# Last recurrent step of a two-layer graph network: gates batch by batch, and half of a batch moved from the TensorE turn to the DRAM path

## The chip, the cores and the metric

The kernel runs on one core of one Trainium2 chip. The metric is the device time of one execution in microseconds; 0.2% of it is about 3.6 us. Names used: PE is TensorE (PEld its weight loads), DVE is VectorE, ACT is ScalarE, SP is the engine whose queue issues every DMA of this kernel.

## The reference

Sixteen batches of 1024 nodes with 128 features go through two layers. The second layer is a gated recurrent update with five steps. Everything is float32. Cut to what matters here:

```python
# layer 1
h = relu(layernorm(x1))
for _ in range(5):
    m = adj @ h                                   # the same matrix for "in" and "out"
    z = sigmoid(concat(m, m) @ w3.T + b3 + h @ u3.T + bu3)
    r = sigmoid(concat(m, m) @ w4.T + b4 + h @ u3.T + bu3)
    hv = tanh(concat(m, m) @ w5.T + b5 + (r * h) @ u5.T + bu5)
    h = (1 - z) * h + z * hv
out = x1 + h
```

x1 is layer 0's output, kept in DRAM until it is needed for the last line.

## The kernel before

**Tiling.** Sixteen batches are worked on in four quads of four (batches 0 to 3, ..., 12 to 15). Two quads are in flight at any time, and each step of one quad has two stages. The aggregation `m = adj @ h` (`aggregate`, matmuls on L504) goes through all four batches at once, with sums that save multiplications. Then come the gates (`gates`, L799), on transposed data: features lie on the 128 partitions, nodes run along the row. A unit is one batch's half of 512 nodes. `hT` holds the state h transposed, `mT` the aggregated messages transposed.

**Gates.** They run for a pair of batches at a time: pair A is the first two batches of a quad, pair B the last two. For a pair's four units, first all four r gates (products with W4A and U3, sigmoid, `r * h` on DVE), then all four z gates (one more product into the same PSUM bank, sigmoid), then the four updates `update` (L835: products with W5A and U5, tanh, then DVE). Without `finish` an update takes three DVE operations: `hv - h`, times z, plus h. All products are issued on L808, with 512 columns; each shows as two pieces in the trace.

**Order.** Every instruction goes through `pin`, so each engine works in exactly the order in which the program is written. `put(key, piece)` hangs a piece of other work on a named place, and `place(key)` runs it there. Places of an aggregation are the numbers 1 to 49 (after so many of its products), those of the gates have names such as `Ar0` or `Bz3`: pair, gate, unit. Loads and stores hung on places go into SP's queue in that order. An SP entry that must wait, for data or for a free buffer, holds up all that stands behind it.

**The last step.** Nothing follows it, so the state is added to x1 and stored. It has two ways from transposed to natural layout:

- Through DRAM: DVE transposes 32x32 squares within the partitions (L669, tile `sq`), one 512 KB store writes them to a scratch (`fn<-sq`), four loads of 128 KB fetch the blocks in natural order (`ho<-fn`, `natural_from`), and DVE adds the blocks to x1 (`xt<-xt,ho`, L241, two strided additions). Batches 12 and 13 (pair A) go this way. `final_outputs` (L1009) puts the loads and the additions in pair B's places: loads at Br0 and Br2, additions with the store to `out` at Bz1 and Bz3.
- By TensorE: `finish` (L1027) multiplies 128 columns of `hT` at a time by the identity (L1043, tile `pf`), and DVE adds the bank to x1. Batches 14 and 15 (pair B) go this way. In pair B `1 - z` is computed as a second sigmoid (L831), and `(1 - z) * h` is done during the z gates (L832), so that an update needs only two DVE operations. The last unit's update is split in two halves of 256 columns.

`flip` has three buffers (`sq`, `ho`), `pre` has four (x1 tiles), `ps_g` four PSUM banks; `ps_m` has tag a with two, b and c with one. Output 11, of the quad before, also lands in this step: its load at Ar0, its addition at Az1, its store at Az2. The x1 loads of batches 12 to 15 sit at Ar1, Ar2, Ar3 and Br1.

Of the kernel before, what the change touches and what calls it, by code (L numbers as in the profile page):

```python
# [8 lines left out]
F32 = mybir.dt.float32  # L9
# [4 lines left out]
P = 128  # L14
# [82 lines left out]
def tile_two_gnn_layers(  # L97
# [30 lines left out]
    def dma(out, in_):  # L128
        pin(nc.sync.dma_start(out=out, in_=in_))

    def by_slots(ap):
        return ap.rearrange("(p c) d -> p c d", c=NC)
# [33 lines left out]
    def flat(t):  # L166
        names = "abcd"[: len(t.shape) - 1]
        return t.rearrange(f"p {' '.join(names)} -> p ({' '.join(names)})")
# [68 lines left out]
    def sub(o, a, b):  # L237
        pin(nc.vector.tensor_sub(o, a, b))  # L238

    def add(o, a, b):  # L240
        pin(nc.vector.tensor_add(o, a, b))  # L241
# [405 lines left out]
    def scratch_for(kind, nm):  # L647

        scratch = dram.tile([P, N], F32, tag=f"{kind}_{nm}", name=f"{kind}_{nm}")
        return scratch, scratch.rearrange("(a y) (k f) -> k y a f", a=NSQ, k=NSQ)  # L650
# [4 lines left out]
    def flip_tile(nm):  # L655
        return flip.tile([P, NSQ, NC, SQ], F32, tag="sq", name=nm)

    def squares_of_half(sq, g):
        return sq[:, :, bass.ts(g, CH), :].rearrange("p k j e -> p j k e")

    def transposed_half(hT, g):
        return hT[:, bass.ts(g, HALF)].rearrange("p (j k e) -> p j k e", j=CH, k=NSQ)
# [10 lines left out]
    def natural_from(blocks, hN):  # L673

        for k in range(NSQ):
            dma(by_blocks(hN, k), blocks[k])
# [31 lines left out]
    def put(k, *pieces):  # L708
        fixed.setdefault(k, []).extend(pieces)

    def place(k):
        for piece in fixed.pop(k, ()):
            piece()
# [82 lines left out]
        return rest  # L796


    def gates(mT, hT, nm, key, then, finish=None):  # L799

        def view(t, u):
            return t[u[0]][:, bass.ts(u[1], HALF)]

        def multiply(bank, w, moving, start, stop):
            pin(
                nc.tensor.matmul(  # L808
                    bank, w_sb[:, w, :], moving, start=start, stop=stop, skip_group_check=True
                )  # L810
            )

        banks, rh, z = {}, {}, {}
        for k, u in enumerate(UNITS):
            tag = f"{nm}_{u[0]}{u[1]}"
            pg = ps_g.tile([P, HALF], F32, tag="pg", name=f"pr_{tag}")
            multiply(pg, W4A, view(mT, u), True, False)
            multiply(pg, U3, view(hT, u), False, True)
            r = work.tile([P, HALF], F32, tag="r", name=f"r_{tag}")
            pin(nc.scalar.activation(r, pg, AF.Sigmoid, bias=bsum[:, 1:2]))  # L820
            pin(nc.vector.tensor_mul(r, r, view(hT, u)))
            banks[u], rh[u] = pg, r
            place(f"{key}r{k}")
        for k, u in enumerate(UNITS):
            multiply(banks[u], W3A, view(mT, u), False, True)
            tag, h = f"{nm}_{u[0]}{u[1]}", view(hT, u)
            z[u] = work.tile([P, HALF], F32, tag="z", name=f"z_{tag}")
            pin(nc.scalar.activation(z[u], banks[u], AF.Sigmoid, bias=bsum[:, 0:1]))
            if finish:
                rest = work.tile([P, HALF], F32, tag="hv", name=f"rest_{tag}", bufs=3)  # L830
                pin(nc.scalar.activation(rest, banks[u], AF.Sigmoid, bias=nb3, scale=-1.0))  # L831
                pin(nc.vector.tensor_mul(h, h, rest))  # L832
            place(f"{key}z{k}")

        def update(u, part):  # L835

            tag = f"{nm}_{u[0]}{u[1]}_{part.start}"
            h = view(hT, u)[:, part]
            pg = ps_g.tile([P, HALF], F32, tag="pg", name=f"pv_{tag}")[:, part]
            multiply(pg, W5A, view(mT, u)[:, part], True, False)  # L840
            multiply(pg, U5, rh[u][:, part], False, True)
            hv = work.tile([P, HALF], F32, tag="hv", name=f"hv_{tag}", bufs=3)[:, part]
            pin(nc.scalar.activation(hv, pg, AF.Tanh, bias=bsum[:, 2:3]))
            if finish:
                pin(nc.vector.tensor_mul(hv, hv, z[u][:, part]))
            else:
                pin(nc.vector.tensor_sub(hv, hv, h))
                pin(nc.vector.tensor_mul(hv, hv, z[u][:, part]))
            pin(nc.vector.tensor_add(h, h, hv))

        if not finish:
            for k, u in enumerate(UNITS):
                update(u, slice(0, HALF))
                if k % NH == NH - 1:
                    then(u[0])
            return
        updates = [(u, slice(0, HALF)) for u in UNITS[:-1]]
        updates += [(UNITS[-1], slice(k * BLK, (k + 1) * BLK)) for k in range(2)]
        for k, (u, part) in enumerate(updates):
            update(u, part)  # L860
            if k >= 2:
                finish(*updates[k - 2])
        for late in updates[-2:]:
            finish(*late)


    state = {}
# [9 lines left out]
    def step(i, loads_at=(period(4), period(5), "Ar0", "Ar2"), early_places=GATE_PLACES):  # L877
# [24 lines left out]
        if final:  # L902
            st["x1"] = []

            def load_x1(k):
                x1 = x_tile(f"1_{quad * Q + k}")
                dma(x1, x1s[quad * Q + k])
                st["x1"].append(x1)

            for k, places in enumerate(((None, 10, 13), (12, 24, 27), (26, 39, 41), ("Ar0", "Az1", "Az2"))):  # L910
                for piece, at in zip(outputs[(quad - 1) * Q + k], places):
                    if at is not None:
                        put(at, piece)
            for k, at in enumerate(("Ar1", "Ar2", "Ar3", "Br1")):
                put(at, lambda k=k: load_x1(k))
        if source is not None:
            loads_of_next(source, loads_at)
# [27 lines left out]
        if last:  # L945
            outputs.update({quad * Q + k: output(quad * Q + k, Later(lambda n, k=k: ready[k][n])) for k in range(Q)})
            if quad == quads - 2:
                put("Bz1", outputs[quad * Q][0])
        for a, key in enumerate("AB"):
            pair = slice(2 * a, 2 * a + 2)  # L950
            if final and a == 1:
                for k, (load, rest) in enumerate(final_outputs(quad, st, stored)):
                    put(f"Br{2 * k}", load)
                    put(f"Bz{2 * k + 1}", rest)
            gates(
                [mT[:, 2 * a + k] for k in range(2)],
                hT[pair],
                f"{nm}{key}",
                key,
                turn(2 * a),  # L960
                finish=finish(quad, hT[pair], st) if final and a == 1 else None,
            )
        if final:
            st["quad"], st["blocks"] = None, None
            return
        st["step"] += 1
        st["blocks"] = [stored[k] for k in range(Q)]
        if last:
# [36 lines left out]

    def h0_of(quad):
        return Later(lambda k: h0_blocks[quad * Q + k])

    def final_outputs(quad, st, stored):  # L1009
        for k in range(2):  # L1010
            box = {}

            def load(k=k, box=box):
                box["h"] = flip_tile(f"ho_{quad * Q + k}")
                natural_from(stored[k], box["h"])

            def rest(k=k, box=box):
                x1 = st["x1"][k]
                view = x1.rearrange("p j (a e) -> p a j e", e=SQ)
                for g in range(NH):  # L1020
                    js = bass.ts(g, CH)
                    add(view[:, :, js], view[:, :, js], box["h"][:, :, js])
                dma(by_slots(out[quad * Q + k]), x1)

            yield load, rest

    def finish(quad, hT, st):  # L1027

        count = [0]

        def run(u, part):
            i, g = u
            x1 = st["x1"][2 + i]
            n = (part.stop - part.start) // P
            first = g * CH + part.start // P
            bank = ps_m.tile(
                [P, n, D], F32, tag="abac"[count[0] % 4], name=f"pf_{i}_{first}",
                bufs=2 - count[0] % 2,
            )
            count[0] += 1  # L1040
            for j in range(n):
                pin(
                    nc.tensor.matmul(  # L1043
                        bank[:, j, :], hT[i][:, bass.ts(first + j, P)], ident, start=True, stop=True
                    )
                )
            slots = slice(first, first + n)
            add(x1[:, slots], bank, x1[:, slots])
            dma(by_slots(out[quad * Q + 2 + i])[:, slots], x1[:, slots])

        return run


    firsts = [slotwise(nat[:, k]) for k in range(Q)]
# [163 lines left out]
```

## Time and profile before

| what | value |
|---|---|
| median of 3 runs | 1781.39 us (1778.98 to 1782.17) |
| the profiled execution | 1784.15 us |
| its span on the core | 1782.4 us, mean granted clock 0.998 |
| first product of the last step's gates | 1732.04 us |
| last addition on DVE ends | 1779.14 us |

All times below and in the prediction are microseconds from the start of the span. The last step's gates and outputs fill the final 50 us, in which the engines were busy as follows (PE, DVE and ACT, in us):

| stretch | PE | DVE | ACT | granted clock |
|---|---|---|---|---|
| 1732.04 to 1749.20 (pair A) | 17.16 | 9.97 | 7.93 | 1.00 |
| 1749.20 to 1764.80 (pair B: r, z, three updates' products) | 15.60 | 12.74 | 9.45 | 1.00 |
| 1764.80 to 1770.30 | 0.02 | 2.66 | 0.69 | 0.82 |
| 1770.30 to 1782.40 (turning, last update, last stores) | 8.06 | 6.80 | 0.95 | 0.78 |

The table is read by stretch: PE is full in the first two, and in the last two no engine is.

SP's queue in this step, with the start of each entry (an entry that waits starts when its wait ends):

| start | entry |
|---|---|
| 1718.80 to 1721.76 | last three ring loads of the aggregation |
| 1724.86 | store of output 10 |
| 1725.25 | four loads of output 11's blocks |
| 1727.51 to 1729.84 | x1 of batches 11 to 14 |
| 1741.75 | store of output 11 |
| 1750.56 | scratch store of batch 12 |
| 1755.99 | scratch store of batch 13 |
| 1756.40 to 1758.14 | four loads of batch 12's blocks |
| 1758.66 | x1 of batch 15 |
| 1759.09 to 1760.51 | four loads of batch 13's blocks |
| 1763.19, 1768.93 | stores of outputs 12 and 13 |
| 1773.51, 1776.31, 1778.48, 1778.90, 1779.38 | stores of outputs 14 and 15, in parts |

### The profile page before, as it was taken

What the parts mean: (1) busy time and instruction counts of PE and PEld (TensorE: products, weight loads), DVE (VectorE), ACT (ScalarE), POOL (GpSimd) and SP (SyncE); (2) the same over time, 40 slices, a digit from 0 to 9 for tenths busy, and PEclk for the clock granted to TensorE, in tenths of its full rate; (3) what the DMA queues carried; (4) which work ended last, traced back from release to release, by engine and by line L of the source; (5) the groups of instructions that cost most, each with busy time, mean ns of one, the idle gap of its engine ahead of it and who ended that gap; (6) DMA issues with size and microseconds to landing.
All of it is one profiled execution on the core that took longest, in us unless ns stands there. A gap on an engine that the chain in (4) does not pass through costs nothing.

```text
span 1782.4 us, 21452 instructions
## 1 busy us (share of the span) xinstructions
PE 1764.8 (99%) x6450; PEld 1204.2 (68%) x6450; DVE 1372.3 (77%) x2807; ACT 902.4 (51%) x1971; POOL 59.3 (3%) x41
## 2 busy tenths in 40 slices
PE   9999999999999999999999999999999999999997
PEld 4557666588586675858866758576675857658574
DVE  6778979777879688887697968768677776867776
ACT  5246555544555565554455554544445454544543
POOL 3101000000000000000000000000000000000000
PEclk9999999999999999999999999999999999999999
DMA  7489886589495865849849668594775948567593
GB/s 253 158 310 308 238 247 211 179 233 266 120 307 187 270 210 180 260 132 278 253 152 283 212 202 277 164 303 156 221 232 158 295 142 260 189 205 249 162 318 118
DMA packets 168866, 396.36 MB, mean 222 GB/s; under 512 B 18480, under 2 KB 86960, under 8 KB 168752
## 3 DMA queue, kind: packets, MB, share of 16 engines
q1 hardware_dynamic: 168752, 395.00, 70.7%
q8 instruction: 52, 0.85, 0.2%
q14 instruction: 62, 0.51, 0.1%
HBM read 314.18 MB, written 80.74 MB: 222 GB/s over the span
## 4 chain that ended last, share of the span: by engine, by line
PE 84%; DVE 7%; DMA 6%; POOL 1%; ACT 1%; issue 1%; SPq 0%; DVEq 0%; POOLq 0%
PE a L504 23%; PE c L504 12%; PE b L504 6%; DMA ring<-rd 4%; PE a_a L504 3%; PE pr_3B L808 2%; PE pr_2B L808 2%; PE pr_1B L808 2%; PE pr_2A L808 2%; PE pr_1A L808 2%; PE pr_3A L808 2%; PE pr_0B L808 2%; PE pr_4A L808 2%; PE pr_0A L808 2%; PE a_a L620 2%; PE pv_3B L808 2%
## 5 line engine op out<-in xcount | busy, mean ns | idle before, releaser
L504 PE MATMUL a<-ring,big 128*128 128x256 f32 x1120 | 288.3, 380 | 2.9 <-ACT Z L523 2.1
L523 ACT COPY Z<-a 128x256 f32<-128x256 f32 x480 | 177.6, 371 | 196.4 <-PE a L504 196.1
L241 DVE TENSOR_TENSOR Z<-Z,taps 128x512 f32<-128x512 f32 (+1 forms) x264 | 144.6, 554 | 167.1 <-ACT taps L523 166.8
L504 PE MATMUL c<-ring,little 128*128 128x256 f32 x960 | 246.8, 379 | 0.7 <-ACT Z L523 0.5
L504 PEld LDWEIGHTS a<-ring,big 128*128 128x128 f32 x1120 | 211.6, 190 | 41.9 <-issue 8.1
L241 DVE TENSOR_TENSOR mT<-mT,Z 128x1024 f32<-128x1024 f32 x154 | 188.4, 1223 | 24.7 <-ACT Z L523 19.4
L504 PEld LDWEIGHTS c<-ring,little 128*128 128x128 f32 x960 | 181.8, 190 | 27.0 <-ACT Z L523 1.7
L523 ACT COPY taps<-c 128x256 f32<-128x256 f32 x280 | 103.7, 370 | 117.1 <-PE c L504 111.9
L504 PE MATMUL b<-ring,big 128*128 128x256 f32 x560 | 143.8, 379 | 0.4 <-DMA ring<-rd 0.4
L504 PE MATMUL a<-resident,little 128*128 128x256 f32 x560 | 143.9, 379 | 0.0
L504 PE MATMUL a<-ring,little 128*128 128x256 f32 x560 | 143.7, 379 | 0.0
L504 PEld LDWEIGHTS b<-ring,big 128*128 128x128 f32 x560 | 106.3, 190 | 15.2 <-DMA ring<-rd 0.8
L504 PEld LDWEIGHTS a<-resident,little 128*128 128x128 f32 x560 | 106.2, 190 | 14.9 <-ACT Z L523 0.3
L504 PEld LDWEIGHTS a<-ring,little 128*128 128x128 f32 x560 | 106.4, 190 | 14.5
L669 DVE STREAM_TRANSPOSE sq<-hT_all 128x512 f32<-128x512 f32 x156 | 101.2, 686 | 0.0
L401 ACT COPY big<-nat 128x512 f32<-128x512 f32 x132 | 80.6, 614 | 0.1
L523 ACT COPY taps<-b 128x256 f32<-128x256 f32 x140 | 52.1, 372 | 55.5 <-PE b L504 54.6
L238 DVE TENSOR_TENSOR little<-little,big 128x256 f32<-128x256 f32 x154 | 65.4, 425 | 6.7
L238 DVE TENSOR_TENSOR little<-big 128x256 f32<-128x256 f32 x154 | 64.3, 417 | 0.0
L238 DVE TENSOR_TENSOR little<-big,little 128x256 f32<-128x256 f32 x154 | 64.2, 417 | 0.0
L241 DVE TENSOR_TENSOR little<-big 128x256 f32<-128x256 f32 x154 | 64.0, 415 | 0.3 <-ACT big L401 0.2
L523 ACT COPY mT<-a 128x256 f32<-128x256 f32 x80 | 29.8, 372 | 48.1 <-PE a L504 47.9
(267 smaller groups left out, 2915.0 us busy)
## 6 DMA issues: line engine op xcount, KB each, us to landing
ring<-rd SPq DMA_DIRECT2D x440, 512.0 KB, 6.3
fn<-sq SPq DMA_DIRECT2D x78, 512.0 KB, 3.5
nat<-fn SPq DMA_DIRECT2D x256, 128.0 KB, 6.6
x1d<-xt SPq DMA_DIRECT2D x16, 512.0 KB, 5.3
sqt<-ft SPq DMA_DIRECT2D x16, 512.0 KB, 6.5
xt<-x1d SPq DMA_DIRECT2D x16, 512.0 KB, 7.1
xt<-in_x_dram SPq DMA_DIRECT2D x15, 512.0 KB, 4.6
ho<-fn SPq DMA_DIRECT2D x56, 128.0 KB, 6.9
```

The source lines that it names most:

```text
L238: pin(nc.vector.tensor_sub(o, a, b))
L241: pin(nc.vector.tensor_add(o, a, b))
L401: return [lambda i=i: pin(nc.scalar.copy(made_of(k, i), part(a, b, i))) for i in range(2)]
L504: nc.tensor.matmul(bank, l, right[:, c, :], start=opens and c == 0, stop=c == SB - 1, skip_group_check=True,)
L523: pin(nc.scalar.copy(to, bank))
L620: nc.tensor.matmul(bank, left[:, c, :], right[c // SB][:, c % SB], start=p in (1, 2, 5) and c == 0, stop=c == CH - 1, skip_group_check=True,)
L669: pin(nc.vector.transpose(squares_of_half(sq, g), transposed_half(hT, g)))
L808: nc.tensor.matmul(bank, w_sb[:, w, :], moving, start=start, stop=stop, skip_group_check=True)
```

## The change

The last step of the last quad no longer uses `gates`, `finish` and `final_outputs` but a function of its own, `last_gates`. `gates` keeps only the case without `finish`; its other uses are the same instructions as before.

- The order is batch by batch rather than pair by pair: r of batch 12, z of batch 12, r of batch 13, update of batch 12, z of 13, update of 13, then r and z of 14, its update, r and z of 15, its update. Between r and z of batch 15 stand no other products.
- All four batches compute `1 - z` as a second sigmoid and `(1 - z) * h` right after z, so all updates have two DVE operations. The result of that sigmoid goes to `nat`, which is free by then.
- Batches 12 and 13 and the first half of batch 14 go through DRAM. The half takes one transpose, one scratch store of 256 KB in 512-byte pieces and four loads of 64 KB, also in 512-byte pieces. The second half of 14 and both halves of 15 are turned by TensorE, after the last update; the last update is not split.
- The update's banks come from `ps_m`, the turned banks from `ps_g`.
- Output 11's load moves from Ar0 to place 37 of the aggregation, its addition to R10 and its store to R11. The x1 loads go to R00, R01, Z01 and V10.

On SP the order becomes: ring loads, four loads of output 11 and its x1, store of output 10, x1 of 12, 13 and 14, store of output 11, scratch store of 12, x1 of 15, four loads of 12, scratch store of 13, four loads of 13, scratch store of 14's half, store of output 12, four loads of 14's half, store of output 13, two stores of output 14, three of output 15.

```diff
+    def last_gates(quad, hT, x1s):
...
+        def r(k, g):
+            bank = ps_g.tile([P, HALF], F32, tag="pg", name=f"pr_last_{k}{g}")
+            multiply(bank, W4A, columns(mT[:, k], g), True, False)
+            multiply(bank, U3, columns(hT[k], g), False, True)
+            t = work.tile([P, HALF], F32, tag="r", name=f"r_last_{k}{g}")
+            pin(nc.scalar.activation(t, bank, AF.Sigmoid, bias=bsum[:, 1:2]))
+            pin(nc.vector.tensor_mul(t, t, columns(hT[k], g)))
+            banks[k, g], rh[k, g] = bank, t
+            place(f"R{k}{g}")
+
+        def one_z(k, g):
+
+            multiply(banks[k, g], W3A, columns(mT[:, k], g), False, True)
+            z[k, g] = work.tile([P, HALF], F32, tag="z", name=f"z_last_{k}{g}")
+            rest = columns(flat(nat[:, k]), g)
+            pin(nc.scalar.activation(z[k, g], banks[k, g], AF.Sigmoid, bias=bsum[:, 0:1]))
+            pin(nc.scalar.activation(rest, banks[k, g], AF.Sigmoid, bias=nb3, scale=-1.0))
+            h = columns(hT[k], g)
+            pin(nc.vector.tensor_mul(h, h, rest))
+            place(f"Z{k}{g}")
+
+        def update(k, g):
+            tag = "abac"[(2 * k + g) % 4]
+            bank = ps_m.tile([P, HALF], F32, tag=tag, name=f"pv_last_{k}{g}", bufs=2 if tag == "a" else 1)
+            multiply(bank, W5A, columns(mT[:, k], g), True, False)
+            multiply(bank, U5, rh[k, g], False, True)
+            hv = work.tile([P, HALF], F32, tag="hv", name=f"hv_last_{k}{g}", bufs=3)
+            pin(nc.scalar.activation(hv, bank, AF.Tanh, bias=bsum[:, 2:3]))
+            pin(nc.vector.tensor_mul(hv, hv, z[k, g]))
+            add(columns(hT[k], g), columns(hT[k], g), hv)
+            place(f"V{k}{g}")
...
+        def leave(k, gs):
+            sq = flip_tile(f"sq_last_{k}")
+            for g in gs:
+                pin(nc.vector.transpose(squares_of_half(sq, g), transposed_half(hT[k], g)))
+            scratches[k] = scratch_for("fn", f"last_{k}")
+            dma(
+                scratches[k][0].rearrange("p (k f) -> p k f", k=NSQ)[:, :, part(gs)],
+                sq.rearrange("p k j e -> p k (j e)")[:, :, part(gs)],
+            )
+
+        def fetch(k, gs):
+            ho[k] = flip_tile(f"ho_last_{k}")
+            for n in range(NSQ):
+                dma(by_blocks(ho[k], n)[:, :, part(gs)], scratches[k][1][n][:, :, part(gs)])
...
+        def join(k, gs):
+            for g in gs:
+                js = bass.ts(g, CH)
+                x1 = x1s[k].rearrange("p j (a e) -> p a j e", e=SQ)
+                add(x1[:, :, js], x1[:, :, js], ho[k][:, :, js])
+            store(k, slice(gs[0] * CH, (gs[-1] + 1) * CH))
+
+        def turned(k, first, n):
+
+            bank = ps_g.tile([P, n, D], F32, tag="pg", name=f"pf_{k}_{first}")
+            for j in range(n):
+                pin(
+                    nc.tensor.matmul(
+                        bank[:, j, :], hT[k][:, bass.ts(first + j, P)], ident, start=True, stop=True
+                    )
+                )
+            slots = slice(first, first + n)
+
+            def rest():
+                add(x1s[k][:, slots], bank, x1s[k][:, slots])
+                store(k, slots)
+
+            return rest
...
+        every(r, 0)
+        every(one_z, 0)
+        every(r, 1)
+        every(update, 0)
+        leave(0, both)
+        every(one_z, 1)
+        every(update, 1)
+        fetch(0, both)
+        leave(1, both)
+        every(r, 2)
+        every(one_z, 2)
+        fetch(1, both)
+        update(2, 0)
+        leave(2, (0,))
+        update(2, 1)
+        every(r, 3)
+        join(0, both)
+        every(one_z, 3)
+        fetch(2, (0,))
+        join(1, both)
+        update(3, 0)
+        join(2, (0,))
+        update(3, 1)
+        rests = [turned(2, CH, CH), turned(3, 0, CH), turned(3, CH, SB), turned(3, CH + SB, SB)]
+        for rest in rests:
+            rest()
...
-            for k, places in enumerate(((None, 10, 13), (12, 24, 27), (26, 39, 41), ("Ar0", "Az1", "Az2"))):
+            for k, places in enumerate(((None, 10, 13), (12, 24, 27), (26, 39, 41), (37, "R10", "R11"))):
...
-            for k, at in enumerate(("Ar1", "Ar2", "Ar3", "Br1")):
+            for k, at in enumerate(("R00", "R01", "Z01", "V10")):
```

In `last_gates` the batches 12 to 15 are numbered 0 to 3, and g is the half.

More of the change, by code (lines that the diff above doesn't have):

```diff
@@ L796, in put_statistics, with gates @@
         return rest
-    def gates(mT, hT, nm, key, then, finish=None):
+    def gates(mT, hT, nm, key, then):
         def view(t, u):
@@ L828, in gates @@
             pin(nc.scalar.activation(z[u], banks[u], AF.Sigmoid, bias=bsum[:, 0:1]))
[L829 to L832, printed above, removed]
             place(f"{key}z{k}")
[L835 to L842, printed above, removed]
-            pin(nc.scalar.activation(hv, pg, AF.Tanh, bias=bsum[:, 2:3]))
[L844 to L864, printed above, removed]
+        for k, u in enumerate(UNITS):
+            tag, h = f"{nm}_{u[0]}{u[1]}", view(hT, u)
+            pg = ps_g.tile([P, HALF], F32, tag="pg", name=f"pv_{tag}")
+            multiply(pg, W5A, view(mT, u), True, False)
+            multiply(pg, U5, rh[u], False, True)
+            hv = work.tile([P, HALF], F32, tag="hv", name=f"hv_{tag}", bufs=3)
+            pin(nc.scalar.activation(hv, pg, AF.Tanh, bias=bsum[:, 2:3]))
+            sub(hv, hv, h)
+            pin(nc.vector.tensor_mul(hv, hv, z[u]))
+            add(h, h, hv)
+            if k % NH == NH - 1:
+                then(u[0])
@@ new lines, in last_gates, with multiply, columns, part @@
+    def last_gates(quad, hT, x1s):
+        def multiply(bank, w, moving, start, stop):
+            pin(
+                nc.tensor.matmul(
+                    bank, w_sb[:, w, :], moving, start=start, stop=stop, skip_group_check=True
+                )
+            )
+        def columns(t, g):
+            return t[:, bass.ts(g, HALF)]
+        banks, rh, z = {}, {}, {}
+        scratches, sq, ho = {}, {}, {}
+        def r(k, g):
[26 more added lines that the diff above has]
+            place(f"V{k}{g}")
+        def part(gs):
+            return slice(gs[0] * CH * SQ, (gs[-1] + 1) * CH * SQ)
+        def leave(k, gs):
[11 more added lines that the diff above has]
+                dma(by_blocks(ho[k], n)[:, :, part(gs)], scratches[k][1][n][:, :, part(gs)])
+        def store(k, slots):
+            dma(by_slots(out[quad * Q + k])[:, slots], x1s[k][:, slots])
+        def join(k, gs):
[7 more added lines that the diff above has]
+            for j in range(n):
+                pin(
+                    nc.tensor.matmul(
+                        bank[:, j, :], hT[k][:, bass.ts(first + j, P)], ident, start=True, stop=True
+                    )
+                )
+            slots = slice(first, first + n)
[3 more added lines that the diff above has]
+            return rest
+        both = range(NH)
+        def every(what, k):
+            for g in both:
+                what(k, g)
+        every(r, 0)
[24 more added lines that the diff above has]
+            rest()
@@ L948, in step @@
                 put("Bz1", outputs[quad * Q][0])
+        if final:
+            last_gates(quad, hT, st["x1"])
+            st["quad"], st["blocks"] = None, None
+            return
         for a, key in enumerate("AB"):
             pair = slice(2 * a, 2 * a + 2)
[L951 to L954, printed above, removed]
             gates(
@@ L960, in step @@
                 turn(2 * a),
-                finish=finish(quad, hT[pair], st) if final and a == 1 else None,
             )
-        if final:
-            st["quad"], st["blocks"] = None, None
-            return
         st["step"] += 1
@@ L1007, in h0_of @@
         return Later(lambda k: h0_blocks[quad * Q + k])
[L1009 to L1051, printed above, removed]
     firsts = [slotwise(nat[:, k]) for k in range(Q)]
```

## The prediction

> **What bounds the kernel now.** I first read the page's busy row and its chain of work that ended last.
>
> ```profile
> PE 1764.8 (99%) x6450; PEld 1204.2 (68%) x6450; DVE 1372.3 (77%) x2807; ACT 902.4 (51%) x1971; POOL 59.3 (3%) x41
> PE 84%; DVE 7%; DMA 6%; POOL 1%; ACT 1%; issue 1%; SPq 0%; DVEq 0%; POOLq 0%
> ```
>
> TensorE sets the time nearly everywhere. The change reaches only the last step, so I took the chain from 1690 us on, then from 1756 us on (start, length, what):
>
> ```profile
> 1732.20 10.30 PE pr_4A L808 x24
> ...
> 1758.14 0.43 SPq L129
> ...
> 1760.51 6.97 DMA ho<-fn
> ...
> 1767.61 1.29 DVE xt L241 x2
> 1768.90 0.61 DVE hv_4B L845
> ...
> 1770.37 2.04 PE pf L1043 x8
> 1772.42 1.71 PE pv_4B L808 x4
> 1774.12 1.43 PE pf L1043 x8
> 1775.55 0.86 PE pv_4B L808 x4
> 1776.42 1.35 PE pf L1043 x12
> 1777.77 1.37 DVE xt L241 x3
> ```
>
> The chain leaves PE: VectorE, in order, sits in the addition of batch 13's fetched blocks until their loads have landed (1767.5), and every later update of the state queues behind it. The waits of 1732 to 1782 give the price (total, times, longest), and the busy times by stretch show the clock (third figure from the end: granted PE clock):
>
> ```profile
> PE pf L1043 <- DVE hT_all L849: 5.8, 2, 5.6
> DVE xt L241 <- DMA ho<-fn: 4.8, 2, 3.2
> ...
> 1764.80:1768.30 3.50, 0.02 (x1) 0.00 (x0) 0.69 (x2) 0.69 (x1) 0.00 (x0) 1.00 0.46 156
> 1768.30:1775.10 6.80, 4.73 (x18) 4.40 (x19) 5.51 (x9) 0.47 (x1) 0.00 (x0) 0.50 0.29 116
> 1775.10:1779.20 4.10, 3.34 (x24) 2.88 (x23) 3.26 (x7) 0.47 (x1) 0.00 (x0) 1.00 0.17 64
> ```
>
> PE stands still from 1764.8 to 1770.37 and then works at half clock until 1775.1, which about doubles its products (four pieces of a 256-column product 1.71 us, later 0.86).
>
> **The sum, part by part.** I lay the new order on the engines with these rows. A 128x512 product: 10.30 us / 24 pieces, two pieces each, 0.858. A gate on ScalarE starts 0.20 after its product's slot ends; its result is there 0.72 later, a following independent one starts 0.57 later. VectorE 128x512: 0.61 before an independent, 0.73 before a dependent one; 0.65 for a block transpose or a strided addition. The same model run over the old order reproduces VectorE's starts to 0.1 us up to 1763 (first subtraction 1744.98, second batch's transposes ending 1755.9), so I trust it to that.
>
> PE. Before and after, eight halves take five products each, 40 x 0.858 = 34.3 us from 1732.04. Going batch by batch, two z products wait about 0.06 us each for ScalarE to have read the bank; the last update's products end at 1766.55. The old order had the same work, but the 5.57 us wait and the half clock inside it. Turning three halves instead of four takes four 128-column products off.
>
> ScalarE gains four sigmoids (1 - z of batches 12 and 13): 4 x 0.57 = 2.3 us. They lie beside the products of the next halves; ScalarE was busy 19.0 of the last 50.4 us. If that cover were gone, tanh would be up to 0.6 late in each of two places. VectorE loses four subtractions and gains four products with 1 - z: nil, and these come before tanh. The fifth transpose and the seventh strided addition add 1.30, one addition from PSUM goes (-0.69).
>
> Output 11's load moves ahead (place 37 instead of the gates), past output 10's store in SP's queue. Five loads (1 MB) then stand right behind the last three ring loads instead of 3.5 us later. The ring loads are ahead of them in the one queue, so I take 0; the second of those three lands at 1727.09 and is used at 1727.72, so sharing could cost up to about 0.5. Its addition to output 11 (2 x 0.65) stays in VectorE's slack at 1740.5, where it is today.
>
> The DRAM legs, in SP's order. Batch 12: update done 1746.4, transposes to 1747.7, store issued 1747.7, landing 2.6 later (the store issued at 1750.56 landed at 1753.13), batch 15's x1 load between, four loads issued 1750.3 to 1752.2, due on VectorE only at 1762.9. Covered by 7 us even with the 7.0 us of today's slow one. Batch 13: store 1752.9, loads 1755.5 to 1757.3, due 1765.4: covered. So today's wait disappears. Behind the store of batch 13 on SP stands the half store of batch 14 (transposed at 1758.6, issued 1759.2); behind it the store of output 12, which waits for VectorE; and **behind that** the four loads of batch 14's half. This is what is late next: they reuse the buffer that output 12's addition frees.
>
> - r of the last half ends on PE at 1761.35; +0.20 +0.72 = 1762.27; its product with h 0.61 = 1762.88.
> - Output 12's two additions, 1.30: 1764.2. Its store is issued, then four half-size loads, first 1764.6, fourth 1.5 later, 1766.1.
> - Meanwhile VectorE does two (1 - z) h (1.22), output 13's additions (1.30), the third-last update (0.73 + 0.61): idle from 1768.1.
> - Landing. The nearest row is the set whose fourth load was issued at 1758.14, also behind a 512 KB write: VectorE got it at 1761.87, 3.73 later. So 1766.1 + 3.7 = 1769.8. VectorE waits 1.7 us.
> - Then batch 14's half addition 0.65, the last update 0.73 + 0.61, four additions from PSUM 0.63 + 0.63 + 0.42 + 0.47: 1773.9. The turning products hide beside these.
> - The end: 3.26 us lay between VectorE's last end (1779.14) and the span's end: 1777.2. Against 1782.4: **-5.2 us**.
>
> Bounds of that landing. Below: half the bytes in 512-byte pieces, perhaps 1768.1 or earlier, no wait, -6.9. Above: the slow set, issued at 1760.51 and landing 6.97 later; but it had a 512 KB load and another set in front, and nothing such is in front here, so I stay with 3.7; the high end would be 1773.1 and -1.9.
>
> **Two rules weighed.** The row for a small load behind a write is 3.73 us. The Trainium skill, "DMA: Bandwidth & Descriptors", section on the anatomy of one DMA, gives a fit (for the other, GpSimd path) of about 2.0 us plus bytes over 436 GB/s: 2.15 us for 64 KB, landing at 1768.3, a wait of 0.2 and -6.7. Its rules for kernel authors add, against this change, that transfers around 64 KB and less are mostly overhead: halving the bytes of such a set does not halve its time. With four queued loads behind a write I keep the row.
>
> The clock: the row above shows half clock from 1768.3, 3.5 us after PE fell idle, for 6.8 us. "TensorE: Matmul & The Clock Gate", Part 1 on the clock gate, says one idle window of about 3.4 us does that. In my order PE's longest gap is from 1769.1 to 1771.8, 2.7 us, just short: full clock by the rule, and the last eight 128-column pieces take about 1.1 us. If the window (free-running, by that page) catches it, they take some 2 us, +0.7. That side goes into the range.
>
> **How this stands to the times.** The profiled execution took 1784.15 us with a span of 1782.4; the three runs' median is 1781.39. I take -5.2 off both: 1779.0 for such a profiled run, **1776.2** against the median. What this kernel's measurement can tell from no change is about 0.2%, 3.6 us.
>
> **Rivals.**
>
> 1. The half of batch 14 is the new bound (10%). It lands like today's slow set, and PE goes to half clock in the longer gap: VectorE idles until 1773.1, +0.7 for the clock: span 1781.2, -1.2, about 1780.2. For it: it is issued late, behind a store on SP, in 512-byte pieces of which the trace has none on this path. Against it: queues are otherwise quiet.
> 2. No wait at all (17%): the half lands by 1768.1. VectorE then bounds the end: 1772.2 + 3.26 = 1775.5, -6.9, about 1774.5. For it: the fit above; half the bytes. Against it: the 3.3 us that the quickest load of such a set took from issue to landing.
> 3. Slower than before (5%): one mechanism, batch 14's half through DRAM in 512-byte pieces. Its store has 512 pieces where a full store has 128, and the loads must wait for it on SP. It decides once the loads land after 1775.0, that is 1769.8 plus the 5.2 us gained. The slowest such load in the whole trace took 9.9 us from issue, which alone gives 1776.0 and a span of 1783.4. If the store, issued at 1759.2, takes 9 us, the loads go out from 1768.2 to 1769.7 and land at 1779.6: span 1787.0, +4.6, about 1786.0. Against it: the store, of half the bytes, would need three times what the whole 512 KB stores of this stretch took (2.6 and 2.9).
> 4. The change doesn't do what it says: the ring loads, delayed by the loads put behind them, push the gates back by up to 2 us (4%): -3.2, about 1778.2.
>
> **Chances and range.** Forecast (a wait of 0.5 to 3 us at batch 14's half) 64%, rivals 10, 17, 5 and 4. Faster by over 0.2% needs -3.6: the forecast but 1, rival 2 and half of rival 4: 0.82. Within 0.2%: rival 1 and half of 4: 0.12. Slower: rival 3, and 1 of the forecast for scatter between runs: 0.06. The range from 1773.5 (rival 2 less 1 for scatter) to 1780.3 (rival 1) leaves out rival 3 and the tails.
>
> **What would show it.** Right: no wait of PE over 1 us between 1732 and the last update's products, granted clock 1.00 up to there, the fetched batches 12 and 13 added without a DMA wait, one DMA wait of 1 to 2 us on VectorE at output 14's half, VectorE's last addition near 1773.9, span near 1777. Wrong: a PE wait on the ring around 1727 that moves the first gate past 1732.5; z products waiting more than 0.3 us for ScalarE; VectorE waiting at output 12 or 13; the half's loads more than 6 us from issue to landing; clock 0.50 before the last products.

## The result, and the profile after

| | before | changed |
|---|---|---|
| median | 1780.97 us (7 runs, 1778.98 to 1784.03) | 1775.84 us (7 runs, 1771.35 to 1779.16) |
| ratio | | 0.997 (95% interval 0.9956 to 0.9983) |
| profiled execution, its span | 1784.15, 1782.4 us | 1779.16, 1777.4 us |
| first gate product of the last step | 1732.04 us | 1733.80 us |
| DVE's last addition ends | 1779.14 us | 1774.68 us |
| tail: from the one to the other | 47.10 us | 40.88 us |

The kernel is faster by 0.3%, 5.1 us by the medians. The **tail**, from the first gate product of the last step to the end of DVE's last addition, measures the changed part alone; the start of the gates scatters from one execution to the next by several us (1725.8 to 1733.8 us in the thirteen profiles of this study), and nothing changed acts on most of what lies ahead of it.

The busy row and the chain of the changed kernel's page, to be held against those before:

```profile
PE 1761.9 (99%) x6438; PEld 1200.4 (68%) x6438; DVE 1372.8 (77%) x2806; ACT 903.7 (51%) x1974; POOL 59.3 (3%) x41
PE 89%; DMA 5%; DVE 4%; ACT 1%; POOL 1%; issue 0%; SPq 0%; DVEq 0%; POOLq 0%
```

PE has more of the chain and DVE less (89 and 4% where it was 84 and 7). The chain's end, from 1757 us on (start, length, what):

```profile
1756.66 3.43 PE pv_last L850 x8
1760.09 3.45 PE pr_last L850 x8
...
1764.89 1.30 DVE xt L241 x2
...
1768.37 2.04 DMA ho_last<-fn_last
...
1770.49 0.69 DVE xt L241
1771.18 0.61 DVE hv_last L889
...
1771.82 0.70 DVE hT_all L241
...
1772.65 1.58 PE pf L927 x8
...
1774.26 0.42 DVE xt L241
```

Read from below: the last addition waited for the last turned columns, these for the last update, that for the addition of batch 14's half, and this for its loads, which stand on SP behind output 12's store. It is the chain that the prediction drew. Its waits, from 1732 us on (total, times, longest):

```profile
PE pf L927 <- DVE hT_all L241: 1.7, 2, 1.3
...
DVE xt L241 <- DMA ho_last<-fn_last: 0.4, 1, 0.4
DVE xt L241 <- PE pf L927: 0.2, 1, 0.2
```

No wait stops PE by more than 1.34 us before its last eight pieces, where one had stopped it for 5.57. DVE from 1764.3 us on (the bracket is the idle time ahead of a row):

```profile
1764.28 0.69 DVE L867 TENSOR_TENSOR r_last<-r_last,hT_all 128x512 f32<-128x512 f32 x1 [1.02 <-ACT r_last L866]
1764.89 1.29 DVE L241 TENSOR_TENSOR xt<-xt,ho_last 128x512 f32<-128x512 f32 x2
1766.09 1.47 DVE L879 TENSOR_TENSOR hT_all<-hT_all,nat 128x512 f32<-128x512 f32 x2
1767.48 1.29 DVE L241 TENSOR_TENSOR xt<-xt,ho_last 128x512 f32<-128x512 f32 x2
...
1770.49 0.69 DVE L241 TENSOR_TENSOR xt<-xt,ho_last 128x512 f32<-128x512 f32 x1 [0.39 <-DMA ho_last<-fn_last]
```

The additions of batches 12 (1764.89) and 13 (1767.48) have no bracket: their loads had landed 8.4 and 5.7 us before. From here to 1774.68 DVE waits for other engines and loads only 0.39 and 0.23 us. The new bound of the end is DVE's own queue. The stretches around the last products (length, then busy time of PE, PEld, DVE, ACT and POOL; the third figure from the end is the granted clock):

```profile
1771.30:1772.65 1.35, 0.01 (x1) 0.03 (x1) 1.31 (x3) 0.00 (x0) 0.00 (x0) 1.00 0.44 173
1772.65:1774.70 2.05, 1.57 (x8) 1.27 (x8) 1.81 (x4) 0.00 (x0) 0.00 (x0) 0.63 0.41 157
```

The clock fell to half at 1773.2, in the midst of the last eight pieces, though PE's longest stop was 1.34 us. And ahead of the gates, PE at the aggregation's last ring loads (`ring<-rd`, 512 KB each):

```profile
1727.21 1.13 PE L504 MATMUL b<-ring,big 128*128 128x256 f32 x4 [1.02 <-DMA ring<-rd]
...
1729.41 1.10 PE L504 MATMUL a<-ring,big 128*128 128x256 f32 x4 [0.20 <-DMA ring<-rd]
```

Before, there had been one such wait:

```profile
1725.89 1.13 PE L504 MATMUL b<-ring,big 128*128 128x256 f32 x4 [0.39 <-DMA ring<-rd]
```

### The profile page after: what moved, and what is told of

It is laid out like the page before. It is cut to its first block, busy times and chain, and to the rows that moved or that the text cites. A ratio compares the mean times of both kernels' runs of the same rounds, so it can differ in the third digit from the quotient of the medians.

```text
span 1777.4 us, 21433 instructions
## 1 busy us (share of the span) xinstructions
PE 1761.9 (99%) x6438; PEld 1200.4 (68%) x6438; DVE 1372.8 (77%) x2806; ACT 903.7 (51%) x1974; POOL 59.3 (3%) x41
## 4 chain that ended last, share of the span: by engine, by line
PE 89%; DMA 5%; DVE 4%; ACT 1%; POOL 1%; issue 0%; SPq 0%; DVEq 0%; POOLq 0%
PE a L504 25%; PE c L504 12%; PE b L504 6%; PE a_a L504 3%; DMA ring<-rd 3%; PE pr_3B L808 2%; PE pr_1B L808 2%; PE pr_0B L808 2%; PE pr_2B L808 2%; PE pr_2A L808 2%; PE pr_1A L808 2%; PE pr_0A L808 2%; PE pr_3A L808 2%; PE a_a L620 2%; PE pv_0B L808 2%; PE pv_3B L808 2%
```

## The experiments

Eleven kernels ran, one of them the changed kernel once more. The ratio is to the kernel before on the same chip, with its 95% interval; the ring wait is PE's, for the last three ring loads ahead of the gates. Tail and ring wait are of one profile each. Five profiles whose tails should agree (changed, e1, e7, e9, e11) gave 40.51 to 40.88 us, so a difference of 0.4 in one tail means little.

| kernel | median, us | ratio | tail, us | ring wait, us |
|---|---|---|---|---|
| before | 1780.8 to 1781.58 | 1 | 47.10 | 0.39 |
| changed | 1775.84 | 0.9970 (0.9956 to 0.9983) | 40.88 | 1.22 |
| e1 load 11 late | 1775.16 | 0.9964 (0.9950 to 0.9979) | 40.53 | 0.25 |
| e2 before, load 11 early | 1782.59 | 1.0006 (0.9997 to 1.0016) | 45.97 | 1.56 |
| e3 before, addition late | 1775.92 | 0.9967 (0.9953 to 0.9981) | 41.33 | 1.33 |
| e4 turn four | 1776.25 | 0.9975 (0.9965 to 0.9986) | 40.09 | 2.24 |
| e5 additions early, load 11 late | 1773.84 | 0.9957 (0.9945 to 0.9970) | 39.31 | 0 |
| e6 pair order | 1778.03 | 0.9986 (0.9977 to 0.9995) | 43.23 | 0.93 |
| e7 subtract in two | 1773.45 | 0.9953 (0.9939 to 0.9966) | 40.52 | 0 |
| e8 as e5, turn four | 1772.87 | 0.9954 (0.9941 to 0.9968) | 39.69 | 0.31 |
| e9 changed, again | 1776.00 | 0.9972 (0.9961 to 0.9983) | 40.51 | 1.72 |
| e10 e5 and e7 | 1774.29 | 0.9961 (0.9949 to 0.9974) | 39.31 | 0 |
| e11 e7, load 11 late | 1774.83 | 0.9968 (0.9955 to 0.9981) | 40.62 | 0 |

### What was paid before: one addition late (e3)

The kernel before, with the addition of batch 13's blocks hung behind the third update of pair B.

```diff
             update(u, part)
+            place(f"{key}u{k}")
             if k >= 2:
...
-                    put(f"Bz{2 * k + 1}", rest)
+                    put(("Bz1", "Bu2")[k], rest)
```

> The kernel before with one edit: the addition of batch 13's fetched blocks goes behind the third update of the last pair instead of ahead of the first. Nothing else of the change is in it: pairs, subtraction in pair A, four turned halves. Theory A (what was paid is that VectorE, in order, stood at the load with all updates behind it, and PE then ran at half clock): the addition finds its data landed, PE doesn't stop, granted clock 1.00 up to the last update, tail 42.2 instead of 47.1 us, about 0.3% faster than before. Theory B (the gain of the change comes from going batch by batch and from sending the batches off earlier): tail 45 us or more, gain at most 2 us.

DVE in this kernel, from the first addition of fetched blocks on:

```profile
1760.36 1.29 DVE L241 TENSOR_TENSOR xt<-xt,ho 128x512 f32<-128x512 f32 x2 [1.33 <-DMA ho<-fn]
1761.58 1.28 DVE L832 TENSOR_TENSOR hT_all<-hT_all,rest_4B 128x512 f32<-128x512 f32 x2
1762.78 0.68 DVE L845 TENSOR_TENSOR hv_4B<-hv_4B,z_4B 128x512 f32<-128x512 f32 x1
...
1766.76 1.29 DVE L241 TENSOR_TENSOR xt<-xt,ho 128x512 f32<-128x512 f32 x2
```

PE at its first turned columns, where it had stood still for 5.57 us before:

```profile
1764.34 1.13 PE L1044 MATMUL pf<-ident,hT_all 128*128 128x128 f32 x8 [0.77 <-DVE hT_all L849]
```

The updates (1762.78) now run ahead of batch 13's addition (1766.76), which has no wait any more; batch 12's still waits 1.33. PE's stops for the state are three of at most 0.77 us, the clock stays full to the last product, and the tail is 41.3, which is theory A's 42.2 less 0.9. Times and interval are those of the whole change. So the blocked queue, with the half clock that followed it, was what the old order paid, and this one edit takes the whole of it back.

### What the order by batches is worth (e6)

The changed kernel with r of both batches, z of both, then the updates:

```diff
+        every(r, 2)
+        every(r, 3)
+        fetch(1, both)
+        join(0, both)
+        every(one_z, 2)
+        every(one_z, 3)
+        update(2, 0)
+        leave(2, (0,))
+        fetch(2, (0,))
...
```

> The changed kernel's last step in the old order by pairs: r of both batches, z of both, then both updates; the early product with 1 - z, the half of batch 14 through DRAM and the late turning stay. Output 12's addition stands ahead of the last pair's z gates. Theory A (the order by batches is worth what it brings batch 14's half forward, some 5 us earlier on its way): VectorE waits about 1.7 us for that half, tail about 42 us against 40.9. Theory B (the order by batches is the gain of the change): tail 45 us or more. Theory C: the order is worth nothing, 40.9.

DVE, the half of batch 14, and PE, the last products:

```profile
1768.79 0.69 DVE L241 TENSOR_TENSOR xt<-xt,ho_last 128x512 f32<-128x512 f32 x1 [2.10 <-DMA ho_last<-fn_last]
```

```profile
1766.84 1.13 PE L927 MATMUL pf<-ident,hT_all 128*128 128x128 f32 x8 [1.22 <-DVE hT_all L241]
1770.96 2.05 PE L927 MATMUL pf<-ident,hT_all 128*128 128x128 f32 x8 [2.99 <-DVE hT_all L241]
```

Theory A, with a longer tail than it said (43.2 us, about 42 expected): the half comes late, DVE waits 2.10 us for it (1.7 expected), and with PE idle for 2.99 the last products run at half clock (2.05 us where full clock took 1.13). The median is 2 us above the changed kernel's. That the order matters only through this half is likely but not shown: e3 keeps the pairs, turns the half on TensorE and has a tail of 41.3, yet it differs from e6 in other points too.

### Whether the third leg through DRAM is worth anything (e4, e8)

```diff
-        leave(2, (0,))
...
-        fetch(2, (0,))
...
-        join(2, (0,))
...
-        rests = [turned(2, CH, CH), turned(3, 0, CH), turned(3, CH, SB), turned(3, CH + SB, SB)]
+        rests = [turned(2, 0, CH), turned(2, CH, CH), turned(3, 0, CH), turned(3, CH, SB), turned(3, CH + SB, SB)]
```

> The changed kernel with batch 14 turned by TensorE as a whole: no transpose, no store, no loads and no strided addition for its first half, four more 128-column products and one more addition from PSUM. Theory A (the third leg through DRAM is no gain in itself; VectorE has the same count of additions and the leg costs a transpose and a wait of 0.39 us): tail 40.3 us against 40.9, no difference that the times show. Theory B (two and a half batches through DRAM are needed because PE or the additions from PSUM bound the end): tail 41.5 us or more.

DVE at the end of e4:

```profile
1765.75 0.69 DVE L241 TENSOR_TENSOR hT_all<-hT_all,hv_last 128x512 f32<-128x512 f32 x1
1766.36 0.68 DVE L889 TENSOR_TENSOR hv_last<-hv_last,z_last 128x512 f32<-128x512 f32 x1
1767.08 0.69 DVE L241 TENSOR_TENSOR hT_all<-hT_all,hv_last 128x512 f32<-128x512 f32 x1
1767.68 2.54 DVE L241 TENSOR_TENSOR xt<-pf,xt 128x512 f32<-128x512 f32 x5
```

The last update follows the one before without a wait, and five additions from PSUM run in a piece: tail 40.1, 0.4 to 0.8 less than with the leg (40.51 and 40.88). Theory A; in the times no difference (the intervals overlap). e8 asks the same with the additions of batches 12 and 13 moved up, as in e5 below:

> As the run with the additions moved up, but with batch 14 turned by TensorE as a whole, so without the third leg through DRAM. Theory A (the leg is no gain): tail 38.5 to 39.5 us, like the other within 0.7. Theory B (once VectorE is no longer the bound, the 1 us of products and the addition from PSUM that the leg saves count): 0.6 to 1 us longer than the other.

Its tail is 39.7 against e5's 39.3 (theory A: within 0.7), its ratio the same within the intervals. The leg is no gain that shows in either setting.

### The early product with 1 - z in two more batches (e7, e10, e11)

```diff
-            pin(nc.scalar.activation(rest, banks[k, g], AF.Sigmoid, bias=nb3, scale=-1.0))
-            h = columns(hT[k], g)
-            pin(nc.vector.tensor_mul(h, h, rest))
+            if k >= 2:
+                pin(nc.scalar.activation(rest, banks[k, g], AF.Sigmoid, bias=nb3, scale=-1.0))
+                h = columns(hT[k], g)
+                pin(nc.vector.tensor_mul(h, h, rest))
...
+            if k < 2:
+                sub(hv, hv, columns(hT[k], g))
             pin(nc.vector.tensor_mul(hv, hv, z[k, g]))
```

> The changed kernel with batches 12 and 13 updated in the old way, subtraction, product with z, addition, without the second sigmoid and the early product; the rest as changed. Theory A (worth nothing: ScalarE had room and VectorE has the same number of operations): tail 40.9 within 0.4 us, no difference in the times. Theory B (the longer update delays the scratch stores and so the end): tail 41.5 us or more.

The tail, 40.5, is theory A's. The median was 2.4 us below the changed kernel's, which theory A doesn't give, so it was run again in two more settings beside the changed kernel on one chip:

> The run with the additions moved up (output 11's load late), and batches 12 and 13 updated by subtraction as before. Theory A (the early product in these two batches is worth nothing, and the additions moved up are worth 1.5 us): tail 39.3 us within 0.4, 1 to 2 us faster than the changed kernel. Theory B (the subtraction is what made the run with it as fast): 0.15% faster than the run with the additions moved up alone, about 0.9942.

> The changed kernel with subtraction in batches 12 and 13 and output 11's load at the first gate. Theory A (neither is worth anything that the times show): tail 40.5 us, time within 0.1% of the changed kernel on the same chip. Theory B (subtraction gains 0.17% as the earlier pair of medians has it, 1773.45 against 1775.84): 3 us faster than the changed kernel.

1774.29 and 1774.83 beside 1776.00, with tails of 39.31 (e5's own) and 40.62: subtraction does nothing to the tail that shows, and e11's ratio (0.9968) is the changed kernel's (0.9972). e10 is not faster than e5. The good median of e7 was not found again.

### Output 11's load, put behind the ring loads (e1, e2, e9)

```diff
-            for k, places in enumerate(((None, 10, 13), (12, 24, 27), (26, 39, 41), (37, "R10", "R11"))):
+            for k, places in enumerate(((None, 10, 13), (12, 24, 27), (26, 39, 41), ("R00", "R10", "R11"))):
```

> The changed kernel with output 11's load at the first gate instead of place 37 of the aggregation. In the changed kernel's profile PE waited 1.02 + 0.20 us for the last ring loads and the gates began at 1733.80 us, against 0.39 us and 1732.04 before. Theory A (the early load, put right behind the ring loads, shares the engines with them): these waits fall back to about 0.4 us in total, the ring load that took 9.25 us to land takes about 7.2 again, and the kernel gains 0.8 us. Theory B (the later start is scatter between executions; the queue is served in order): waits of 0.4 to 1.3 us as it falls out, no gain. Tail from the first gate product to VectorE's last end unchanged by both, 40.9 us.

e2 is the counterpart, `"Ar0"` to `37` in the kernel before:

> The kernel before with nothing but output 11's load moved to place 37. Theory A: PE waits about 1.2 us for the last ring loads instead of 0.39, the time rises by 0.8 us. Theory B: 0.4 us as before, no difference. The tail stays at 47.1 us by both.

e9 is the changed kernel itself:

> The changed kernel itself once more, on the same chip as the two that follow. In its first profile PE waited 1.2 us for the last ring loads and its last eight products ran at half clock (1.57 us instead of about 1.1). Theory A (both are scatter: where the free-running clock window and the queue happen to stand): a tail of 40.4 to 40.9 us, the ring wait anything from 0 to 1.5 us, time about 0.3% below before. Theory B (the early load of output 11 costs about 1 us each time): ring wait over 1 us again.

PE's waits for the ring, first in e1, then in e2, then in e9:

```profile
1724.11 1.13 PE L504 MATMUL b<-ring,big 128*128 128x256 f32 x4 [0.25 <-DMA ring<-rd]
```

```profile
1721.72 1.13 PE L504 MATMUL b<-ring,big 128*128 128x256 f32 x4 [0.89 <-DMA ring<-rd]
1724.38 1.10 PE L504 MATMUL a<-ring,big 128*128 128x256 f32 x4 [0.67 <-DMA ring<-rd]
```

```profile
1722.23 1.13 PE L504 MATMUL b<-ring,big 128*128 128x256 f32 x4 [0.73 <-DMA ring<-rd]
1725.22 1.10 PE L504 MATMUL a<-ring,big 128*128 128x256 f32 x4 [0.99 <-DMA ring<-rd]
```

The second row is the telling one. A wait for the second of the last three ring loads stands in five of the six profiles with the early load (changed, e2, e4, e6, e9; not e7) and in none of the seven with the late one: 0.44 us on average against 0. That load took 8.2 us on average from issue to landing in the six and 7.0 in the seven. The third took 9.1 to 10.7 us in the six and 7.2 to 7.9 in six of the seven (9.7 in e3), but PE never waited for it.

All ring waits together average 1.28 us with the early load (1.22, 1.56, 2.24, 0.93, 0, 1.72) and 0.33 with the late one (0.39, 0.25, 1.33, 0, 0.31, 0, 0). Of this difference of 0.95 us, the other half belongs to the first of the three loads, which landed after 8.3 and 8.1 us on average, hardly later; that the early load is its cause is not shown. So theory A holds for about 0.4 us, with much scatter between executions. The times alone would not have shown it: e2's +0.06% has an interval from -0.03 to +0.16.

Both theories of e2 had its tail at 47.1 us, and it was 45.97. Batch 13's last load landed 6.1 us after its issue there, 7.0 in the profile before, so the old order's tail can differ by about 1 us from one execution to the next.

In e9 the last eight products took 1.13 us at full clock, behind a stop of 1.29 us like the first profile's 1.34; the clock fell at 1770.45 us, 0.9 after the last of them. Half clock or not in the same order: here it is scatter, as e9's theory A has it.

### A version with the additions moved up (e5)

```diff
         fetch(1, both)
+        join(0, both)
         update(2, 0)
         leave(2, (0,))
         update(2, 1)
-        every(r, 3)
-        join(0, both)
-        every(one_z, 3)
+        r(3, 0)
         fetch(2, (0,))
         join(1, both)
+        r(3, 1)
+        every(one_z, 3)
         update(3, 0)
```

Output 11's load is late as in e1.

> The changed kernel with output 11's load at the first gate and the additions of batches 12 and 13 moved up in VectorE's order: 12's behind the z gates of batch 14 (its loads had landed at 1756.5), 13's between the two r gates of batch 15, and with them the loads of batch 14's half, which no longer stand behind output 12's store. Theory A (from the last r gate on VectorE is the bound of the end, 10.4 us with 0.6 idle in the changed kernel; taking 2.6 us of additions out of it lets PE's last update set the end): tail 38.5 us against 40.9, no DMA wait on VectorE, faster than the changed kernel by about 2 us, about 0.4% faster than before. Theory B (PE's last update bounds the end already): tail 40 us or more.

DVE at its end:

```profile
1762.97 0.69 DVE L889 TENSOR_TENSOR hv_last<-hv_last,z_last 128x512 f32<-128x512 f32 x1 [0.34 <-ACT hv_last L888]
...
1764.30 0.69 DVE L241 TENSOR_TENSOR xt<-xt,ho_last 128x512 f32<-128x512 f32 x1
1764.90 0.68 DVE L889 TENSOR_TENSOR hv_last<-hv_last,z_last 128x512 f32<-128x512 f32 x1
```

In the last update but one DVE now waits for tanh (0.34), so for PE's products, and not for a load; from there it runs to the end without a stop. The tail is 39.3, between the two theories, 1.6 below the changed kernel's and 1.2 below that of e1, which has the late load too. Of the 0.8 short of 38.5, about 0.3 is the half of batch 14 that still stands between the last two updates: in e8, without it, DVE waits 0.30 for tanh there. e5, e8 and e10 have the shortest tails; e5 and e8 took 0.43 and 0.46% less than before. That they beat the changed kernel is shown by the tail, not by the intervals, which overlap.

## Why the prediction was right, by its own steps

**Sign and size.** Forecast -5.2 us, measured -5.1 by the medians; 1776.2 against 1775.84, span 1777.2 against 1777.4. The mechanism stands: e3 shows that the blocked addition, with the half clock behind it, was the cost. The agreement to a few tenths is luck. In the profiles the tail shrank by 6.2 us and what follows it by 0.5, while the gates began 1.8 us later, which the forecast took at 0.

**The model of the tail.** Forecast from first product to DVE's last end: 1773.9 - 1732.04 = 41.9 us; measured 40.88, and 40.51 in e9. PE's order and DVE's starts came as laid out: DVE done with the last update but one (the prediction calls it the third-last) 36.1 us after the first gate product by forecast, 36.3 measured. "Covered" was right for batches 12 and 13. Its margin for batch 12 was misread, without effect: loads issued by 1752.2 that take 7.0 us land 3.7 us ahead of 1762.9, not 7.

**Term mis-sized: the landing of batch 14's half.** I took 3.73 us from the fourth load's issue to DVE, from a set of twice the size behind a write. The trace has 2.04 us to landing, 2.12 to DVE's start, with the store's own 512 KB ahead all the same. So DVE waited 0.39 us and not 1.7, between the forecast's least, 0.5, and rival 2's none. The row was too long in two ways. With no store in flight ahead, loads of 128 KB took 2.5 to 2.9 us (changed, e5, e6) and not 3.6; and loads of 64 KB took 1.8 to 2.0 (e5, e6), so the size counted for about as much as the rest of the queue. The Trainium skill's fit ("DMA: Bandwidth & Descriptors", anatomy of one DMA), about 2.15 us for 64 KB, was the better guide here than my row; the four loads took 2.57, 2.41, 2.07 and 2.04.

**Step that failed: "The ring loads are ahead of them in the one queue, so I take 0".** Being ahead in the queue did not protect the ring loads from what is issued right behind them: 0.44 us of waiting for the second of the three is shown, inside the 0.5 allowed for sharing and far from rival 4's 2 us. One of the listed signs of being wrong did come: PE waited 1.02 us for the ring at 1727.2, and the first gate stood at 1733.80, past 1732.5. Of the 1.76 us by which it came later, the ring waits make 0.83; 0.69 stood there already ahead of them, and nothing of the change explains that.

**The clock.** Forecast full, with +0.7 if the window catches a gap of 2.7 us. The gap was 1.34 us, and the clock fell all the same in the first profile (1.57 instead of 1.13 us, +0.44), and in e9 only after the last product. The traces show why. In all thirteen, the long stretch of full clock lasted 515 to 518 steps of 3.413 us (1768.10 us in the changed kernel, 1764.69 in e9), and the half clock before the change lasted two (6.83). The rule of "TensorE: Matmul & The Clock Gate" on the free-running window is borne out in this. The plainer reading, that a gap below about 3.4 us is safe, is not: in the 3.41 us before the clock fell, PE had been busy for 1.68 in the changed kernel; in e1 it was busy for 1.72 of such a step, and the clock stayed full. In the last steps of all thirteen traces full clock was kept where PE had 1.72 us of work or more, and lost where it had 1.68 or less: what counted was PE's work in the step, about half of it, and not the longest stop.

**Worth nothing, as costed:** the early product with 1 - z in two more batches (e7, e11). The exchange of a turned half for one through DRAM, which the forecast charged with a transpose and a wait, shows no gain either (e4, e8). Rival 3 (512-byte pieces) is refuted: the store of 512 pieces landed in 2.51 us, less than a full store's 2.6 to 2.9; only its issue took 0.60 us on SP instead of 0.32.

## What to carry to other kernels

An in-order engine that waits for a load pays with everything queued behind it: before regrouping the work, move the one waiting instruction behind the work that is ready; here two changed lines gave the whole gain (e3). Once such a stop is gone, ask which queue is full next (here DVE's last 10 us) and take out what could have run in an earlier gap. A load that is issued early to be safe is not free when it stands right behind the loads that the bound engine is about to use: here it cost about 0.4 us.

## What I had not expected

- Loads issued behind others in one queue slow these: the last ring load took 7.2 us to land before and 9.3 after the move, with 1 MB put right behind it. PE had no need of that one yet; it waited for the load before.
- Small loads are not all overhead: with no store in flight ahead, 64 KB in 512-byte pieces took 1.8 to 2.0 us (e5, e6), 128 KB in 1 KB pieces 2.5 to 2.9. With a 512 KB store in flight ahead, as in the changed kernel, the 64 KB loads still took only 2.0 to 2.6.
- The clock of TensorE can fall with no stop over 1.34 us.
- A 256 KB store in 512-byte pieces took no longer to land than a 512 KB one in 4 KB pieces: 2.5 us against 2.6 to 2.9.
